# A graph layer with 34 wider node updates and some source columns copied on chip

## The chip, the cores and the metric

The kernel runs on one core of a Trainium2 chip. Its engines are TensorE (PE, with its weight load shown as PEld), VectorE (DVE), ScalarE (ACT), GpSimd (POOL) and SyncE (SP, which issues most transfers). The metric is the device time of one execution in microseconds, median of the runs.

## What is computed

A message-passing layer over 12,500 nodes of 64 values and 200,000 edges with 32 values each, in fp32. The edges come sorted by destination; destinations are drawn as 12500·u² with u uniform, so nodes with small numbers have many edges and those with large numbers few.

```python
msg_in = concatenate([nodes[row], nodes[col], edge_features])     # row: source, col: destination
messages = relu(msg_in @ mW1 + mb1) @ mW2 + mb2                   # hidden width 128, result 64
aggregated = segment_sum(messages, col)
upd = relu(concatenate([nodes, aggregated]) @ uW1 + ub1) @ uW2 + ub2
out = layernorm(nodes + upd)
```

## The kernel before

**Tables.** mW1 has three parts, for source, destination and edge. The products of all nodes with the first two are made once, in 13 chunks each: `chunk_a` writes `tab_a` = x·W1a to DRAM (L408 to L422) at the start, and `chunk_b` writes `tab_b` = x·W1b + b1, its first part at the start and the rest within the loop.

**Tiles and groups.** 128 edges are a tile (1563 of them), eight tiles a group (196, counted by `s`), two groups a pair (98, counted by `g`). The loop over `s` is at L583; the order of its work is written out by hand (`tc.manual_schedule()`), and each engine works in the order in which its instructions were issued there.

**What a group costs.** In each step of the loop:

- `gather` (L164, POOL): one indirect DMA per tile fetches 128 rows of 512 bytes of `tab_a` by the edges' sources. There are 14 buffers of a group (`ROWB`), so gathers are issued 14 groups ahead; the gather into a buffer waits for `h` of the group that used it. The first 8 groups (`XG`) gather rows of x instead.
- `windows` (L220, L225, SP): eight DMAs, each 32 rows of `tab_b`, for the destinations of a tile: they are sorted, so those of a tile lie within 32 nodes (`WIN`).
- `edge_part` (L251, PE): for each tile, one matmul adds the edges' own part and the destinations' part, by a stacked operand of 64 rows: edge values, and a 0/1 selection of the window's rows. In fp32 a matmul is shown as two passes.
- `node_part` (L272 DVE, L273 ACT): `h` = relu(pc + xg), eight tiles in one instruction each.
- `collect` (L298, L303, PE): the messages' hidden values are summed over destinations. For each tile `h` times a 0/1 matrix of 32 columns is added into the columns of `sums` at the tile's window, and edges are counted into `cnt`. The place comes from a register, loaded at L294.
- `select`, `load`, `counts`, `loadd` (L190 to L211): the 0/1 matrices for the pair after, and its edge values.

**Node updates.** `sums` covers 384 nodes (`UW`). When the edges of a stretch of nodes are done, an update follows, spread over some steps: `close` copies sums and counts to SBUF (ACT, L317 and L318), `columns` loads the nodes' x columns (SP, L324 and L326), `carry` takes the window that two stretches share over into the next sums (PE, L311 and L312), `update` multiplies to 128 hidden values (PE L333 and L334, ACT L336), `residual` multiplies back and takes the statistics (PE L344 and L345, DVE L349 and L351, ACT L353), `norm` scales (DVE L359 and L362), and `store` writes (SP L368). Which updates there are is fixed ahead by `updates()` from the expected distribution: 54 of them, each ending at a whole pair. `offsets` works out at the start where each tile's window lies in its stretch.

**In case of other data.** A flag is computed from the real destinations (`checks`); where a window or a stretch would be too wide, a slow general path at L627 does everything again.

Of the kernel before, what the change touches and what calls it, by code (L numbers as in the profile page):

```python
# [11 lines left out]
I32 = mybir.dt.int32  # L12
# [28 lines left out]
EARLY = NCH * P  # L41
GE = 20
BS = 8
UB = 3
NCOL = (-(-N // P) + UB) * P
UW = UB * P
ONE = D - 1


def updates():  # L50


    def node(g):
        return N * min(1.0, g * SUP * P / E) ** 2
    at = [0]
    for g in range(1, NSUP):
        if g > at[-1] and node(g + 1) - node(at[-1]) > UB * P - 2 * WIN:
            at.append(g)
    return at


# [1 line left out]


@with_exitstack
def gnn_kernel(ctx: ExitStack, tc: tile.TileContext, x1T, x, eT, e_rows, src, dst, dst_row, wrow, wnext, whalf,
               mW1, mb1, mW2, mb2, uW1, ub1, uW2, ub2, out):

# [35 lines left out]
    past = const.tile([1, 1], F32, name="past")  # L104
    w1b = const.tile([P, DH], F32, name="w1b")
    b1 = const.tile([P, DH], F32, name="b1")

    sums_s = [const.tile([P, UW], F32, name=f"sums_s{k}") for k in range(2)]
    xw = [const.tile([P, UW], F32, name=f"xw{k}") for k in range(2)]
# [21 lines left out]
    cps = cpool.tile([P, WIN + SUP], F32, name="cps")  # L131
    slot = cps[:, :WIN]
    drc = const.tile([P, NT], F32, name="drc")
    flag_i = const.tile([1, 1], I32, name="flag_i")
    usup = const.tile([1, K], I32, name="usup")
    ustep = const.tile([1, K], I32, name="ustep")
# [4 lines left out]

    rows = ctx.enter_context(tc.tile_pool(name="rows", bufs=ROWB))
    xg = {}

    def frees(s):

# [6 lines left out]
    def gather(s):  # L153

        if s >= XG or s % 2 == 0:
            buf = rows.tile([P, SUB, DH], F32, name="xg")
        else:
            buf = xg[s - 1][0]
        if s < XG:
            a = buf.rearrange("p k (b d) -> p (k b) d", d=D)[:, s % 2 * SUB:(s % 2 + 1) * SUB, :]  # L160
        else:
            a = buf.rearrange("p (b k) d -> p k b d", b=2)
        for i, t in enumerate(tiles(s)):
            nc.gpsimd.indirect_dma_start(  # L164
                out=a[:, i, :] if s < XG else a[:, i // 2, i % 2, :], out_offset=None, in_=A[:, :] if s >= XG else x[:, :],
                in_offset=bass.IndirectOffsetOnAxis(ap=src_s[:, t:t + 1], axis=0))
        xg[s] = buf, a

    with tc.tile_pool(name="sup", bufs=2) as sup, tc.tile_pool(name="work", bufs=2) as work, tc.manual_schedule():
# [63 lines left out]
            nc.scalar.copy(xt, pt)  # L233
            xs[s] = xt

        def parts(n):

            if n == SUB:
                return [slice(0, SUB)]
            return [slice(b * SUB // 2, b * SUB // 2 + (n - b + 1) // 2) for b in range(2) if n > b]  # L240

        def edge_part(s):

            n = len(tiles(s))
            g, j = divmod(s, SUP // SUB)
            pc = psum.tile([P, 2, SUB // 2, DH], F32, name="pc")
            for i in range(n):
                k, b = divmod(i, 2)
                q, m = 64 * b, j * SUB // 2 + k

                nc.tensor.matmul(pc[:, b, k, :], L[g][q:q + 64, m, :], rhs[g % 2][q:q + 64, m, :],  # L251
                                 start=s >= XG or k == 0, stop=s >= XG)
            pcs[s] = pc

        def node_part(s):

            n = len(tiles(s))
            pc = pcs.pop(s)
            h = work.tile([P, 2, SUB // 2, DH], F32, name="h")
            if s < XG:  # L260
                xt = xs.pop(s)
                for i in range(n):
                    k, b = divmod(i, 2)
                    q = 64 * b
                    nc.tensor.matmul(pc[:, b, k, :], xt[q:q + 64, k, :], w1a[q:q + 64], start=False,
                                     stop=i + 2 >= n)
                nc.scalar.activation(h, pc, AF.Relu)
            else:
                hf, pf = (t.rearrange("p b k f -> p (b k) f") for t in (h, pc))
                a = xg.pop(s)[0]  # L270
                for m in parts(n):
                    nc.vector.tensor_tensor(hf[:, m], pf[:, m], a[:, m], op=ALU.add)  # L272
                    nc.scalar.activation(hf[:, m], hf[:, m], AF.Relu)  # L273
            hs[s] = h

        def opened(u):
# [37 lines left out]
        def close(u):  # L314

            ps, pn = sums.pop(u)
            nc.scalar.copy(sums_s[u % 2], ps)  # L317
            nc.scalar.copy(xw[u % 2][0:1], pn)  # L318

        us = {}  # L320

        def columns(u):

            n0 = nc.values_load(usup[0:1, u:u + 1], engines=[ET.SP], min_val=0, max_val=N - 1,  # L324
                                skip_runtime_bounds_check_because="destinations are node numbers")
            nc.sync.dma_start(xw[u % 2][ONE:], x1T[:, bass.ds(n0, UW)])  # L326
            us[u] = n0

        def update(u):

            n0 = us[u]
            pu = psum.tile([DH, UW], F32, name="pu", tag="pc")
            nc.tensor.matmul(pu, w2u, sums_s[u % 2], start=True, stop=False)  # L333
            nc.tensor.matmul(pu, uz, xw[u % 2], start=False, stop=True)  # L334
            hT = work.tile([DH, UW], F32, name="hTu", bufs=1)
            nc.scalar.activation(hT, pu, AF.Relu, bias=ub1_s)  # L336
            us[u] = (n0, hT)

        def residual(u):

            n0, hT = us[u]
# [23 lines left out]

        def store(u):
            n0, o = us.pop(u)
            nc.sync.dma_start(out[bass.ds(n0, UW), :].rearrange("(c p) d -> p c d", p=P), o)  # L368


        WCH = 1024

        def relative(a, b):

# [57 lines left out]
        def offsets():  # L432

            nc.vector.memset(usup[:, 0:1], 0)
            wv = wint.rearrange("o (g t) -> o g t", t=SUP)
            ov = woff.rearrange("o (g t) -> o g t", t=SUP)
            k = 0
            while k < K:
                end = UPD[k + 1:] + [NSUP]
# [7 lines left out]
                nc.vector.tensor_tensor(o, w, usup[:, k:k + n].unsqueeze(2).broadcast_to([1, n, d * SUP]),  # L447
                                        op=ALU.subtract)
# [22 lines left out]
        for t in xw:  # L471
# [11 lines left out]
        for k, c in enumerate(range(0, NB, NCH)):  # L483
# [14 lines left out]
            if k == 9:  # L498
                select(0)
                load(0)  # L500
                counts(0)
        columns_of(NCH, nc.sync)

        def rest(s):

            if s == 1:
                relative(8 * SUP, 8 * SUP + WCH)
            elif s == 2:
                relative(8 * SUP + WCH, NT)
                halves(4 * SUP, NTP // 2)  # L510
            elif s == BS:
# [31 lines left out]
        def checks():  # L543
# [17 lines left out]

            uf = work.tile([1, K + 1], F32, name="uf", bufs=1)
            nc.vector.tensor_copy(uf[:, :K], usup)
            nc.vector.memset(uf[:, K:], float(N - WIN))
            gap = work.tile([1, K + 1], F32, name="gap", bufs=1)
            nc.vector.tensor_tensor(gap[:, :K], uf[:, 1:], uf[:, :-1], op=ALU.subtract)
            nc.vector.tensor_scalar(gap[:, :K], gap[:, :K], float(UB * P - WIN), None, op0=ALU.is_gt)
# [4 lines left out]

        due = {SUP // SUB * (UPD[u + 1] if u + 1 < K else NSUP) + 1: u for u in range(K)}
        last = SUP // SUB * NSUP + 1

        period = [max(u for u in range(K) if UPD[u] * SUP <= s * SUB) for s in range(NSUB)]
        transpose(0)
        edge_part(0)  # L580
        gathered = XG
# [1 line left out]
        for s in range(last + 3):  # L583
# [9 lines left out]
                node_part(s)  # L593
            if 1 <= s <= NSUB:
                collect(s - 1)
            if j == 0 and g + 1 < NSUP:
                select(g + 1)
                load(g + 1)
# [190 lines left out]
```

## Time and profile before

| | |
|---|---|
| runs | 2796.53, 2772.33, 2795.54 us; median 2795.54 |
| profiled execution | 2797.45 us, span 2795.7 us |
| instructions counted as work | PE 9558 (and as many weight loads), DVE 1103, ACT 534, POOL 1572 |
| busy share of the span | PE 59%, PEld 51%, DVE 20%, ACT 13%, POOL 53% |
| gathers of `tab_a` (L164) | 1499, 944 ns each, 1415.0 us busy |
| moved | 213.70 MB, 76 GB/s over the span |
| granted TensorE clock | 0.54 of full speed |
| gathers of `tab_a` begin | 138.6 us |

A line of the costliest groups reads: line of the code, engine, operation, output<-inputs, how many; then busy time and mean duration of one in ns; then the idle time of the engine just before them with what ended most of it. "Issue" is time in which the engine waited for nothing that the profile shows. Busy shares are means over the whole span: the start (tables), the long loop with gathers and its last part without gathers have different limits.

### The profile page before, as it was taken

To read this page: it belongs to the slowest core of one execution; us is meant where nothing else is said; L and a number is where in the kernel's file an instruction comes from. 1 tells how busy PE (TensorE), PEld (TensorE's weight loads), DVE (VectorE), ACT (ScalarE), POOL (GpSimd) and SP (SyncE) were. 2 spreads that over 40 slices of the span, in tenths; PEclk is the share of its full clock that TensorE was granted. 3 is DMA by queue.
4 is the path that set the end of the run, shared out by engine and by line. 5 is a ranking of instruction groups with operands and counts; after the bars stand their busy time and mean duration, and the time that the engine had idled before them with its cause. 6 is when DMAs were issued, how large, how long until landed. Compare 5 with 4: busy or idle time off the path is not lost. (4 is left out here: it accounts for less than half of the span.)

```text
span 2795.7 us, 34750 instructions
## 1 busy us (share of the span) xinstructions
PE 1650.0 (59%) x9558; PEld 1427.7 (51%) x9558; DVE 553.1 (20%) x1103; ACT 361.6 (13%) x534; POOL 1476.6 (53%) x1572
## 2 busy tenths in 40 slices
PE   1412755555564646655656655656666676675788
PEld 1312654555454545544546544555555555564667
DVE  0200121222111112111211211212122222221233
ACT  0100101101010111111111111111111111111122
POOL 7175445654555655555555564565555555555510
PEclk6555555555555555555555555555555555555566
DMA  3531233333222222222222222222222222222221
GB/s 89 144 90 51 74 84 91 90 93 85 69 75 67 78 67 73 74 72 72 74 73 74 73 75 71 70 77 76 71 76 66 77 75 75 75 78 73 74 69 44
DMA packets 248063, 213.70 MB, mean 76 GB/s; under 512 B 81153, under 2 KB 213143, under 8 KB 247880
## 3 DMA queue, kind: packets, MB, share of 16 engines
q0 software_dynamic: 50016, 100.44, 14.0%
q1 hardware_dynamic: 182310, 100.72, 13.1%
q10 hardware_dynamic: 15554, 10.31, 1.3%
q8 instruction: 90, 1.47, 0.2%
q14 instruction: 93, 0.76, 0.1%
HBM read 192.55 MB, written 18.68 MB: 76 GB/s over the span
## 5 line engine op out<-in xcount | busy, mean ns | idle before, releaser
L164 POOL DMA_INDIRECT xg<-tab_a,src_s x1499 | 1415.0, 944 | 1183.8 <-DVE h L272 440.6
L251 PE MATMUL pc<-rhs,l 64*128 64x128 f32 x3126 | 531.4, 424 | 677.5 <-issue 411.8
L251 PEld LDWEIGHTS pc<-rhs,l 64*128 64x128 f32 x3126 | 432.1, 306 | 733.9 <-issue 629.4
L298 PEld LDWEIGHTS sums<-sel,h 128*128 128x128 f32 x3126 | 637.2, 301 | 206.6 <-issue 199.8
L298 PE MATMUL sums<-sel,h 128*128 128x32 f32 x3126 | 626.8, 366 | 151.7 <-issue 149.8
L272 DVE TENSOR_TENSOR h<-pc,xg 128x1024 f32<-128x1024 f32 x189 | 228.6, 1210 | 954.5 <-remote 319.5
L273 ACT ACTIVATE h<-h 128x1024 f32<-128x1024 f32 x189 | 197.7, 1047 | 598.9 <-DVE h L272 495.3
L196 DVE TENSOR_TENSOR sel<-cps,drc 128x512 f32<-128x512 f32 x98 | 67.3, 686 | 634.6 <-remote 333.4
L192 DVE TENSOR_TENSOR l<-l,cps 128x1024 f32<-128x1024 int32 (+1 forms) x101 | 123.3, 1221 | 206.0 <-DMA l<-in_dst_row 159.6
L204 ACT CAST selb<-sel 128x512 bf16<-128x512 f32 x98 | 60.4, 616 | 667.4 <-DVE sel L196 398.4
L303 PE MATMUL cnt<-selb,one 128*1 128x32 bf16 x1563 | 95.2, 188 | 51.0 <-issue 50.6
L336 ACT ACTIVATE hTu<-pu,ub_s 128x384 f32<-128x384 f32 x54 | 31.3, 580 | 696.0 <-remote 308.5
L344 PE MATMUL py<-ux,xw 128*128 128x64 f32 x324 | 95.5, 384 | 26.7 <-issue 23.1
L303 PEld LDWEIGHTS <-one 128*1 128x1 bf16 x1563 | 62.7, 83 | 89.7 <-issue 77.5
L345 PE MATMUL py<-u,hTu 128*128 128x64 f32 x324 | 93.9, 382 | 21.1 <-issue 20.7
L344 PEld LDWEIGHTS py<-ux,xw 128*128 128x128 f32 x324 | 77.1, 288 | 34.3 <-issue 28.4
L345 PEld LDWEIGHTS py<-u,hTu 128*128 128x128 f32 x324 | 79.8, 297 | 26.0 <-issue 25.5
L408 PE MATMUL pb<-w1a,xl 64*128 64x128 f32 x196 | 30.6, 430 | 99.6 <-DMA xl<-in_x1T 93.2
L333 PE MATMUL pu<-sums_s,w2u 128*128 128x384 f32 x108 | 88.2, 921 | 1.5 <-ACT sums_s L317 1.5
L408 PEld LDWEIGHTS pb<-w1a,xl 64*128 64x128 f32 x196 | 26.2, 311 | 103.7 <-issue 92.8
L334 PE MATMUL pu<-xw,uz 128*128 128x384 f32 x108 | 73.7, 782 | 0.0
L349 DVE BATCH_NORM_STATS2 st<-py 128x6 f32<-128x64 f32 x162 | 26.6, 220 | 237.6 <-PE py L345 120.3
(86 smaller groups left out, 594.3 us busy)
## 6 DMA issues: line engine op xcount, KB each, us to landing
l<-in_dst_row SPq DMA_DIRECT2D x196, 128.0 KB
l<-in_eT SPq DMA_DIRECT2D x196, 128.0 KB
rhs<-tab_b SPq DMA_DIRECT2D x1563, 16.0 KB
xg<-tab_a,src_s POOLq DMA_INDIRECT x1499
tab_b<-tb SPq DMA_DIRECT2D x13, 512.0 KB
tab_a<-tb ACTq DMA_DIRECT2D x12, 512.0 KB
xw<-in_x1T SPq DMA_DIRECT2D x54, 97.5 KB
out<-o SPq DMA_DIRECT2D x54, 96.0 KB
```

The lines of the kernel that those rows point to most:

```text
L164: nc.gpsimd.indirect_dma_start(out=a[:, i, :] if s < XG else a[:, i // 2, i % 2, :], out_offset=None, in_=A[:, :] if s >= XG else x[:, :], ...
L192: nc.vector.tensor_tensor(l[r], l[r].bitcast(I32), node[r].unsqueeze(2).broadcast_to([r.stop - r.start, SUP // 2, P]), op=ALU.is_equal)
L196: nc.vector.tensor_tensor(s[:, :nt], slot.unsqueeze(1).broadcast_to([P, nt, WIN]), drc[:, g * SUP:g * SUP + nt].unsqueeze(2).broadcast_to( ...
L251: nc.tensor.matmul(pc[:, b, k, :], L[g][q:q + 64, m, :], rhs[g % 2][q:q + 64, m, :], start=s >= XG or k == 0, stop=s >= XG)
L272: nc.vector.tensor_tensor(hf[:, m], pf[:, m], a[:, m], op=ALU.add)
L273: nc.scalar.activation(hf[:, m], hf[:, m], AF.Relu)
L298: nc.tensor.matmul(ps[:, bass.ds(ws[i], WIN)], h[:, i % 2, i // 2, :], S[g][:, k0 + i, :], start=False, stop=ends and i == n - 1)
L303: nc.tensor.matmul(pn[:, bass.ds(ws[i], WIN)], one, SB[g][:, k0 + i, :], start=False, stop=ends and i == n - 1)
L333: nc.tensor.matmul(pu, w2u, sums_s[u % 2], start=True, stop=False)
L334: nc.tensor.matmul(pu, uz, xw[u % 2], start=False, stop=True)
L344: nc.tensor.matmul(py[:, i], xw[u % 2][:, i * P:(i + 1) * P], ux, start=True, stop=False)
L345: nc.tensor.matmul(py[:, i], hT[:, i * P:(i + 1) * P], u2, start=False, stop=True)
```

## The change

Two things are changed.

**Updates.** They cover 448 nodes (`UN`) instead of 384, may end at any group instead of at whole pairs, and there are 34 instead of 54: after groups 35, 49, 60, 69 and so on; every four groups from 128 to 160, every three from there to 193. `sums` and the counts are 480 columns wide (448 and a window), the columns behind are worked on in four blocks of 128, not three. `close` is issued earlier in the step, ahead of `edge_part`.

**Copied tiles.** x, transposed, is kept in SBUF whole (`xcol`, 64 partitions of 12,544 columns, loaded by seven DMAs at the start). In each odd full group from 13 on, 91 groups, the last tile is not gathered. Instead `copies` brings the x columns of its 128 sources one by one into a tile `xo`, 64 in each of two steps: 36 by copies of one column on ACT, 28 by adds of one column and a zero on DVE. Each address is a register value; they are loaded by two multi-register loads on ACT (18 each) and one on DVE (28). `edge_part` then adds xo·W1a for this tile with one more matmul, and `node_part` adds over seven tiles and makes the relu of the eighth directly from `pc`, as an ACT instruction of its own.

```diff
-UB = 3
+CG = 2
+CF = 6 * CG
+CA = 36
+NCT = -(-(NSUB - CF) // CG)
+UB = 4
-UW = UB * P
+UN = 448
+UW = UN + WIN
...
-        for i, t in enumerate(tiles(s)):
+        for i, t in enumerate(tiles(s)[:SUB - copied(s)]):
             nc.gpsimd.indirect_dma_start(
...
+    def copied(s):
+        return s >= CF and s % CG == CG - 1 and len(tiles(s)) == SUB
...
                 nc.tensor.matmul(pc[:, b, k, :], L[g][q:q + 64, m, :], rhs[g % 2][q:q + 64, m, :],
-                                 start=s >= XG or k == 0, stop=s >= XG)
+                                 start=s >= XG or k == 0, stop=s >= XG and not c)
+                if c:
+                    nc.tensor.matmul(pc[:, b, k, :], xo[s // CG % 2][q:q + 64], w1a[q:q + 64], start=False, stop=True)
...
-                for m in parts(n):
+                for m in parts(n, copied(s)):
                     nc.vector.tensor_tensor(hf[:, m], pf[:, m], a[:, m], op=ALU.add)
                     nc.scalar.activation(hf[:, m], hf[:, m], AF.Relu)
+                if copied(s):
+                    nc.scalar.activation(h[:, 1, SUB // 2 - 1], pc[:, 1, SUB // 2 - 1], AF.Relu)
...
+        def copies(s):
+            t = (s + 2) // CG * CG + CG - 1
+            if t < CF or not t < NSUB or not copied(t):
+                return
+            n = P // CG
+            k = (s + 2) % CG * n
+            r = t // CG - CF // CG
+            to = xo[t // CG % 2]
+            def by_dve(o, i):
+                nc.vector.tensor_tensor(o, i, slot[D:, 0:1], op=ALU.add)
+
+            parts = []
+            for a, b, e, copy in ((k, k + CA // 2, ET.Activation, nc.scalar.copy),
+                                  (k + CA // 2, k + CA, ET.Activation, nc.scalar.copy),
+                                  (k + CA, k + n, ET.DVE, by_dve)):
+                _, v = nc.values_load_multi_w_load_instructions(
+                    srow[r:r + 1, a:b], engines=[e], min_val=0, max_val=N - 1,
+                    skip_runtime_bounds_check_because="sources are node numbers")
+                parts += [(copy, a + i, v[i]) for i in range(b - a)]
+            for copy, i, v in parts:
+                copy(to[D:, i:i + 1], xcol[D:, bass.ds(v, 1)])
...
-            nc.sync.dma_start(xw[u % 2][ONE:], x1T[:, bass.ds(n0, UW)])
+            nc.sync.dma_start(xw[u % 2][ONE:, :UN], x1T[:, bass.ds(n0, UN)])
...
+        XCH = 2048
+        def xload(c):
+            e = min(c + XCH, NB * P)
+            nc.sync.dma_start(xcol[D:, c:e], x1T[1:, c:e])
...
                 counts(0)
+                for c in range(0, NB * P, XCH):
+                    xload(c)
...
             if 1 <= s <= NSUB:
                 collect(s - 1)
+            if s + 1 in due:
+                close(due[s + 1])
...
                 chunk_b(chunks.pop(0), [Bv])
+            copies(s)
             if s + 1 < NSUB:
...
-            if s + 1 in due:
-                close(due[s + 1])
             if s + 2 in due:
                 columns(due[s + 2])
```

More of the change, by code (lines that the diff above doesn't have):

```diff
@@ L43, with node @@
 BS = 8
-UB = 3
+CG = 2
[3 more added lines that the diff above has]
+UB = 4
 NCOL = (-(-N // P) + UB) * P
-UW = UB * P
+UN = 448
+UW = UN + WIN
 ONE = D - 1
 def updates():
-    def node(g):
-        return N * min(1.0, g * SUP * P / E) ** 2
+    def node(s):
+        return N * min(1.0, s * SUB * P / E) ** 2
     at = [0]
-    for g in range(1, NSUP):
-        if g > at[-1] and node(g + 1) - node(at[-1]) > UB * P - 2 * WIN:
-            at.append(g)
+    for s in range(1, NSUB):
+        if s > at[-1] and node(s + 1) - node(at[-1]) > UN - WIN:
+            at.append(s)
     return at
@@ L65, in gnn_kernel @@
 @with_exitstack
-def gnn_kernel(ctx: ExitStack, tc: tile.TileContext, x1T, x, eT, e_rows, src, dst, dst_row, wrow, wnext, whalf,
+def gnn_kernel(ctx: ExitStack, tc: tile.TileContext, x1T, x, eT, e_rows, src, src_row, dst, dst_row, wrow, wnext, whalf,
                mW1, mb1, mW2, mb2, uW1, ub1, uW2, ub2, out):
@@ L106, in gnn_kernel @@
     b1 = const.tile([P, DH], F32, name="b1")
+    xcol = const.tile([P, NB * P], F32, name="xcol")
     sums_s = [const.tile([P, UW], F32, name=f"sums_s{k}") for k in range(2)]
-    xw = [const.tile([P, UW], F32, name=f"xw{k}") for k in range(2)]
+    xw = [const.tile([P, UB * P], F32, name=f"xw{k}") for k in range(2)]
+    hT = const.tile([DH, UB * P], F32, name="hTu")
     rhs = [const.tile([P, SUP // 2, DH], F32, name=f"rhs{k}") for k in range(2)]
@@ L133, in gnn_kernel @@
     drc = const.tile([P, NT], F32, name="drc")
+    srow = const.tile([NCT, P], I32, name="srow")
+    xo = [const.tile([P, P], F32, name=f"xo{k}") for k in range(2)]
     flag_i = const.tile([1, 1], I32, name="flag_i")
@@ L234, in transpose, with parts @@
             xs[s] = xt
-        def parts(n):
+        def parts(n, last=False):
             if n == SUB:
-                return [slice(0, SUB)]
+                return [slice(0, SUB - last)]
             return [slice(b * SUB // 2, b * SUB // 2 + (n - b + 1) // 2) for b in range(2) if n > b]
@@ L249, in edge_part @@
                 q, m = 64 * b, j * SUB // 2 + k
+                c = copied(s) and i == n - 1
                 nc.tensor.matmul(pc[:, b, k, :], L[g][q:q + 64, m, :], rhs[g % 2][q:q + 64, m, :],
-                                 start=s >= XG or k == 0, stop=s >= XG)
+                                 start=s >= XG or k == 0, stop=s >= XG and not c)
+                if c:
+                    nc.tensor.matmul(pc[:, b, k, :], xo[s // CG % 2][q:q + 64], w1a[q:q + 64], start=False, stop=True)
             pcs[s] = pc
@@ L317, in close @@
             nc.scalar.copy(sums_s[u % 2], ps)
-            nc.scalar.copy(xw[u % 2][0:1], pn)
+            nc.scalar.copy(xw[u % 2][0:1, :UW], pn)
+        def copies(s):
[18 more added lines that the diff above has]
+                copy(to[D:, i:i + 1], xcol[D:, bass.ds(v, 1)])
         us = {}
@@ L331, in update @@
             n0 = us[u]
[L332 to L337, printed above, removed]
+            pu = psum.tile([DH, UN], F32, name="pu", tag="pc")
+            nc.tensor.matmul(pu, w2u, sums_s[u % 2][:, :UN], start=True, stop=False)
+            nc.tensor.matmul(pu, uz, xw[u % 2][:, :UN], start=False, stop=True)
+            nc.scalar.activation(hT[:, :UN], pu, AF.Relu, bias=ub1_s)
         def residual(u):
-            n0, hT = us[u]
+            n0 = us[u]
             py = psum.tile([P, UB, D], F32, name="py", tag="pc")
@@ L367, in store @@
             n0, o = us.pop(u)
-            nc.sync.dma_start(out[bass.ds(n0, UW), :].rearrange("(c p) d -> p c d", p=P), o)
+            nc.sync.dma_start(out[bass.ds(n0, UB * P), :].rearrange("(c p) d -> p c d", p=P), o)
+        XCH = 2048
         WCH = 1024
+        def xload(c):
+            e = min(c + XCH, NB * P)
+            nc.sync.dma_start(xcol[D:, c:e], x1T[1:, c:e])
         def relative(a, b):
@@ L434, in offsets @@
             nc.vector.memset(usup[:, 0:1], 0)
-            wv = wint.rearrange("o (g t) -> o g t", t=SUP)
-            ov = woff.rearrange("o (g t) -> o g t", t=SUP)
+            wv = wint.rearrange("o (s t) -> o s t", t=SUB)
+            ov = woff.rearrange("o (s t) -> o s t", t=SUB)
             k = 0
             while k < K:
-                end = UPD[k + 1:] + [NSUP]
+                end = UPD[k + 1:] + [NSUB]
                 d = end[0] - UPD[k]
@@ L446, in offsets @@
                 w, o = (v[:, UPD[k]:UPD[k] + n * d].rearrange("o (n d) t -> o n (d t)", n=n) for v in (wv, ov))
-                nc.vector.tensor_tensor(o, w, usup[:, k:k + n].unsqueeze(2).broadcast_to([1, n, d * SUP]),
+                nc.vector.tensor_tensor(o, w, usup[:, k:k + n].unsqueeze(2).broadcast_to([1, n, d * SUB]),
                                         op=ALU.subtract)
@@ L470, in gnn_kernel @@
         nc.vector.memset(zero_b, 0.0)
-        for t in xw:
+        for t in (*xw, hT):
             nc.vector.memset(t, 0.0)
@@ L508, in rest @@
             elif s == 2:
+                nc.sync.dma_start(srow, src_row[CF * SUB + SUB * CG - 1::SUB * CG, :][:NCT])
                 relative(8 * SUP + WCH, NT)
@@ L563, in checks @@
             nc.vector.tensor_copy(uf[:, :K], usup)
-            nc.vector.memset(uf[:, K:], float(N - WIN))
+            nc.vector.memset(uf[:, K:], float(N))
             gap = work.tile([1, K + 1], F32, name="gap", bufs=1)
             nc.vector.tensor_tensor(gap[:, :K], uf[:, 1:], uf[:, :-1], op=ALU.subtract)
-            nc.vector.tensor_scalar(gap[:, :K], gap[:, :K], float(UB * P - WIN), None, op0=ALU.is_gt)
+            nc.vector.tensor_scalar(gap[:, :K], gap[:, :K], float(UN), None, op0=ALU.is_gt)
             nc.vector.tensor_copy(gap[:, K:], past)
@@ L571, in checks @@
             nc.vector.tensor_tensor(flag_i, pf, bad, op=ALU.add)
-        due = {SUP // SUB * (UPD[u + 1] if u + 1 < K else NSUP) + 1: u for u in range(K)}
-        last = SUP // SUB * NSUP + 1
-        period = [max(u for u in range(K) if UPD[u] * SUP <= s * SUB) for s in range(NSUB)]
+        due = {(UPD[u + 1] if u + 1 < K else NSUB) + 1: u for u in range(K)}
+        last = NSUB + 1
+        period = [max(u for u in range(K) if UPD[u] <= s) for s in range(NSUB)]
         transpose(0)
@@ L771 @@
         "src": sp.reshape(-1, P).T[:, :NT],
+        "src_row": sp.reshape(-1, P),
         "dst": dp[:EPAD].reshape(-1, P).T[:, :NT],
```

## The prediction

> **What bounds the kernel now.** I read the costliest groups first, then the table by stretches of time, the waits, and last the timeline of one stretch. Nothing in this program is busy all the time, so the pace has to be found from what waits for what.
>
> ```profile
> L164 POOL DMA_INDIRECT xg<-tab_a,src_s x1499 | 1415.0, 944 | 1183.8 <-DVE h L272 440.6
> L251 PE MATMUL pc<-rhs,l 64*128 64x128 f32 x3126 | 531.4, 424 | 677.5 <-issue 411.8
> L298 PE MATMUL sums<-sel,h 128*128 128x32 f32 x3126 | 626.8, 366 | 151.7 <-issue 149.8
> ```
>
> Here the columns are busy time, mean of one, and idle time before with its releaser. The gathers are the largest single item. A gather lasts 0.944 us and is followed by 0.30 us of issue (timeline below), so one takes 1.245 us and a group of eight takes 10 us. POOL is busy or issuing for about 1415 + 443 = 1858 us. For 440.6 us it waits for h (L272) of the group whose buffer it wants, so POOL is not simply the bound: the wait is closed in a ring from POOL through the arithmetic back to POOL.
>
> ```profile
> core 0: us, PE busy (x) PEld busy (x) DVE busy (x) ACT busy (x) POOL busy (x), PEclk, DMA share, GB/s
> 1100.00:1700.00 600.00, 358.52 (x2008) 313.90 (x2007) 113.98 (x203) 75.72 (x106) 340.31 (x361) 0.52 0.27 73
> 1900.00:2680.00 780.00, 517.07 (x2849) 432.88 (x2849) 171.06 (x420) 118.37 (x196) 419.56 (x446) 0.57 0.28 74
> 2680.00:2776.00 96.00, 95.89 (x698) 79.95 (x696) 40.17 (x103) 28.36 (x49) 1.12 (x2) 0.73 0.23 63
> ```
>
> The last row is the important one: there the gathers have ended. The same table for h alone gives the number of groups in each stretch:
>
> ```profile
> 1100.00:1700.00 600.00, 54.86 (x45) 0.52 0.27 73
> 1900.00:2680.00 780.00, 68.21 (x56) 0.57 0.28 74
> 2680.00:2776.00 96.00, 16.46 (x15) 0.73 0.23 63
> ```
>
> So a group takes 600/45 = 13.3 us, then 780/56 = 13.9 us, and 96/15 = 6.4 us without gathers (I take 6.8, because the first groups of that stretch had been begun before it). The gathers cost the loop about twice what it needs without them. The two stretches with gathers hold 10 and 28 node updates, and differ by only 0.6 us per group.
>
> ```profile
> PEld pc L251 <- issue: 629.4, 395, 21.1
> POOL xg L164 <- issue: 442.6, 1434, 1.0
> POOL xg L164 <- DVE h L272: 440.6, 67, 16.0
> PE pc L251 <- issue: 411.8, 333, 8.1
> ...
> 2618.61 0.37 PE L251 MATMUL pc<-rhs,l 64*128 64x128 f32 x1 [0.22 <-issue]
> 2620.08 0.37 PE L251 MATMUL pc<-rhs,l 64*128 64x128 f32 x1 [1.10 <-issue]
> 2621.55 0.37 PE L251 MATMUL pc<-rhs,l 64*128 64x128 f32 x1 [1.10 <-issue]
> 2619.12 0.94 POOL L164 DMA_INDIRECT xg<-tab_a,src_s  x1 [0.30 <-issue]
> 2625.04 0.71 SPq L326 DMA_DIRECT2D xw<-in_x1T  x1
> ```
>
> The waits give total, times and longest; the timeline gives start, duration, and the idle time in brackets. While gathers run, PE stands still for "issue": its passes come 1.47 us apart, that is 0.71 us for each of the two instructions (weight load and matmul), and SP moves at the same 0.71 us. Reading the timeline through, such slow stretches fill about half of the time while gathers run (some 6.4 us per group), and none comes after the last gather. **The gathers are therefore the bound twice**: by their own pitch and by holding up PE and SP.
>
> **Removed: 91 gathers.** Odd groups from 13 to 193 lose one gather of eight; 91 of 1499. What is one worth? If POOL's pitch counted in full, 1.245 x 91 = 113 us. If POOL would only wait longer for h, nothing. From the table: (13.6 - 6.8)/8 = 0.85 us for each gather of a group, with the effect on PE and SP inside. I take this: 91 x 0.85 = **-77 us**, ends 0 and -113.
>
> **Removed: 20 updates; those left are wider.** An update has 4 blocks, not 3. PE pays L333 and L334 twice each per update, (921 + 782) x 2 = 3.4 us at 384 columns, about 4.0 at 448 by their length, and 6 x 0.38 = 2.3 us of L344 and L345, then 3.1 us. That is 54 x 5.7 = 308 us of PE against 34 x 7.1 = 241 us: 67 us less PE. But the group's time hardly follows the updates: 0.50 against 0.22 per group in the two stretches, and 0.6 us between them, so at most 2.1 us per update; and the stretch of 340 to 1100 us, with 4 updates, takes 13.8 us per group, as much as the last. I take 0.25 us for each: **-5 us**; ends 0 and -67. Moving `close` ahead of edge_part on ACT has one answer: sums are ready there, and its two copies (463 ns each) come before the relu of the next group: nothing. The carried window, the 480 columns of sums and 10 instead of 7 runs of offsets (at the start, small operations of DVE behind the table) are within 2 us together.
>
> **Added: the copies.** For each of 182 groups ACT gets 36 copies of one column and two register loads, DVE 28 adds and one load; besides, each needs its address worked out by the engine's sequencer. The trace has no such copy. Rows that are near: a load of 8 registers (L294) takes 0.59 us, of one (L308) 0.31, so 18 take about 1.0 and 28 about 1.4 us. For ACT the nearest short row is sd, 128x3, 296 ns, which is followed 0.20 us after its start by the next instruction:
>
> ```profile
> 2644.91 0.30 ACT L353 ACTIVATE sd<-mv,eps 128x3 f32<-128x3 f32 x1 [0.62 <-DVE mv L351]
> 2645.11 0.46 ACT L317 COPY sums_s<-sums 128x384 f32<-128x384 f32 x1
> 2645.47 0.46 ACT L318 COPY xw<-cnt 1x384 f32<-1x384 f32 x1
> L351 DVE BATCH_NORM_AGGREGATE mv<-st 128x2 f32<-128x6 f32 x162 | 16.1, 154 | 0.0
> ```
>
> For DVE it is bn_aggr (154 ns, started 0.08 us apart). The address step costs 0.115 us on PE with its matmul (L298) and 0.04 on SP, and can lie beside the copy before. So a copy on ACT costs between 0.10 and 0.32 us; I take 0.15: 36 x 0.15 + 2 x 1.0 = **7.4 us per group** beside the 1.7 us that ACT has (75.72/45). On DVE 0.13: 28 x 0.13 + 1.4 = **5.0 us** beside 2.5 (113.98/45).
>
> [...] No run here shows a copy of one column yet. [...] Their cover is the group's time; past it each microsecond costs 182 us. They are issued ahead of edge_part of the next group and are needed by that (one more matmul in two passes, 0.8 us per two groups, which takes the place of an eighth of the add on DVE) only in the second of the two calls. What stands behind them on ACT and DVE is the relu and the add of the next group, for which POOL and PE wait.
>
> **The tail.** In the last 14 groups, without gathers, the cover is 6.8 us. ACT needs 9.1 for 10 of these groups, about +2 us each, +20; three updates fewer but wider, 8 x 5.7 against 5 x 7.1: -10. Sum **+10 us**.
>
> **The start.** x columns, 64 x 12544 x 4 = 3.2 MB, are loaded by seven DMAs on SP ahead of the loop, where the first 150 us moved 117 GB/s at a DMA share of 0.44. They come beside the rest of the table's writing, and SP's eT load and windows queue behind them. Alone at that rate 27 us; hidden, 0. **+6 us**, ends 0 and 25. SBUF for it (50 KB per partition) has no time.
>
> **Sum**: 2797 - 77 - 5 + 10 + 6 = 2731 against the profiled execution (2797.45, span 2795.7); the median of the runs is 1.9 lower, so **2729 us**, 2.4% faster. Its own range, from the gather's price (-113 to -40) and the start: 2680 to 2775.
>
> **Rivals.**
> *ACT is paced like PE (slower).* ACT would issue about 82 instructions per group, close to PE's 90 (2008 matmuls and as many loads in 45 groups), and PE loses its 6.4 us per group to slow stretches. If these hold ACT too, some 9 instructions pass in 6.3 us at 0.71 us; the rest, 8.5 us by the rows, needs fast time: 6.3 + 8.5 = 14.8 us per group, +1.5 x 182 = +273, and the saved gathers no longer count: about **3075**. With 0.12 per copy it is 2880. It decides as soon as ACT's work exceeds 7.0 us outside the slow stretches. For it: PE and SP both crawl, so it is not one engine's trait. Against it: L351 in its runs of three has 0.0 us idle, and ACT's and DVE's short runs are never torn apart; but none of these is longer than ten, and PE too gets through some 40 instructions before it slows.
> *Gathers were hidden (same).* POOL already waits 440.6 us for h; with 91 x 1.245 us less it would wait 113 us longer, and the copies in the ring DVE-PE-POOL eat the rest: **2795**. Against it: the group's time halves without gathers.
> *Full worth (faster).* -113 and half of the updates' PE (-33), nothing lost at the tail: 2797 - 146 + 6 = **2657**.
> *The change does not do what it says*: with these sources and destinations, no update spans over 448 nodes (the widest step between two starts is 418), so the slow general path at L627 stays out; under 1%.
>
> **Chances.** Forecast 0.40, full worth 0.08, hidden 0.13, ACT paced 0.39. A measurement of this kernel can tell about 1%. Faster 0.46, same 0.13, slower 0.41. The range takes in all of the forecast, most of full worth and two thirds of the slower rival, up to where a copy costs about 0.13 us under slow stretches.
>
> **What would show it.** After the change: POOL x1408 gathers with the same 944 ns; 34 hTu; groups at 12.9 us in 1100 to 1700 us where I am right, 14 and more where ACT is paced. ACT's busy time per group 1.7 to about 7, DVE's 2.5 to about 6. Copies of ACT and DVE in the timeline without gaps of 0.71 us (right) or torn apart by "issue" (the slower rival). POOL's wait for h not over 440 us by more than 50; gathers of tab_a beginning at most 10 us later than 138.6 us. I am wrong if POOL waits for h in place of the gathers saved, or if h waits for ACT's and DVE's copies.

## The result: 5.9% slower, and the profile after

The changed kernel takes **2952.12 us** (2946.04 to 2954.01) against 2789.18, a ratio of **1.059** (1.053 to 1.065). The profiled execution has a span of 2949.3 us. The forecast was 2729 us and faster; what came is between the two figures of the rival "ACT is paced like PE" (2880 and 3075).

The later numbers need one distinction: on some chips, as in this result and in the profile of before, the traces have the slow stretches of 0.71 us per instruction and kernel before takes about 2790 us ("with slow stretches"), and on others the traces have practically none and before takes 1984 us ("without"); what tells them apart isn't known.

The chain of waits that ended last, first of before (by engine; it could be followed back only through the last 500 us), then of the changed kernel, and the changed kernel's costliest groups:

```profile
PE 12%; issue 4%; another core or an unknown queue 2%; DVE 1%; ACT 0%; DVEq 0%; DMA 0%
...
ACTq 35%; issue 27%; ACT 21%; PE 4%; POOL 3%; DVE 3%; another core or an unknown queue 3%; DMA 2%; SPq 1%; DVEq 1%; POOLq 0%
ACTq L355 26%; ACT xo L360 16%; ACTq L360 9%; POOL xg L178 3%; ACT h L290 3%; ACT selb L218 1%; DVE h L289 1%; PE sums L317 1%; PE pc L266 1%; DVE o L402 1%; DMA xl<-in_x1T 1%; SPq L239 1%; ACT sums_s L336 0%; DVE l L206 0%
...
L178 POOL DMA_INDIRECT xg<-tab_a,src_s x1408 | 1328.7, 944 | 1380.6 <-DVE h L289 573.0
L360 ACT COPY xo<-xcol 64x1 f32 x6552 | 750.5, 188 | 1366.9 <-issue 1360.0
L349 DVE TENSOR_TENSOR xo<-xcol,cps 64x1 f32<-64x1 f32 x5096 | 682.8, 159 | 567.1 <-issue 563.8
```

ACT was 13% busy before and had 0% of the chain. Now it and its sequencer (ACTq, which shows 364 register loads at L355 and, for the addresses, 6552 FUSED_REGOPS of 46 ns in the median at L360) hold over half of the chain, and much of "issue" is probably ACT's: the copies (L360) had 1360 us of it ahead of them. The register loads (L355) alone are 26%. POOL saved 86 us of gathers and waits 573.0 us for h (L289; before, L272) instead of 440.6. By stretch: the busy time of all engines, then h alone, whose number is the number of groups, and then what the copies on ACT waited for in each of these stretches (total, times, longest):

```profile
core 0: us, PE busy (x) PEld busy (x) DVE busy (x) ACT busy (x) POOL busy (x), PEclk, DMA share, GB/s
340.00:1100.00 760.00, 412.45 (x2577) 367.46 (x2577) 368.44 (x1839) 315.76 (x2178) 408.95 (x435) 0.51 0.30 80
1100.00:1700.00 600.00, 329.31 (x1987) 289.48 (x1987) 271.12 (x1411) 252.99 (x1702) 305.16 (x324) 0.51 0.25 68
1900.00:2680.00 780.00, 409.16 (x2384) 350.52 (x2386) 319.31 (x1676) 304.35 (x1969) 348.30 (x370) 0.52 0.23 61
...
340.00:1100.00 760.00, 67.28 (x58) 0.51 0.30 80
1100.00:1700.00 600.00, 49.67 (x43) 0.51 0.25 68
1900.00:2680.00 780.00, 57.77 (x50) 0.52 0.23 61
...
ACT xo L360 <- issue: 397.4, 257, 6.3
ACT xo L360 <- issue: 314.4, 236, 5.3
ACT xo L360 <- issue: 424.3, 346, 5.3
```

A group takes 13.1, then 14.0, then 15.6 us (before: 13.8, 13.3, 13.9). Early it is shorter than before, as forecast; then it grows. The waits per group grow with it: 397.4/58 = 6.9, 314.4/43 = 7.3, 424.3/50 = 8.5 us. The timeline of ACT shows what they are made of:

```profile
1406.16 3.02 ACT L360 COPY xo<-xcol 64x1 f32 x29 [1.61 <-issue]
1409.41 0.29 ACT L360 COPY xo<-xcol 64x1 f32 x2 [0.23 <-issue]
1410.10 0.19 ACT L360 COPY xo<-xcol 64x1 f32 x1 [0.40 <-issue]
1410.83 0.29 ACT L360 COPY xo<-xcol 64x1 f32 x2 [0.55 <-issue]
1412.22 0.29 ACT L360 COPY xo<-xcol 64x1 f32 x2 [1.09 <-issue]
```

29 copies go at 0.10 us each, untouched; then single ones and pairs come 0.7 or 1.4 us apart, and DVE's adds at this time do the same (single ones start at 1413.67, 1414.39 and 1415.14 us). Of the 182 runs of 36 copies 151 are torn in this way, 132 of them already after 10 to 19 copies. The sum for ACT per group, from the trace (own work and copies, which are its busy time, the wait ahead of the first copy, which is mostly the loads, and the gaps between copies):

| stretch | own | copies | loads | gaps | sum | group |
|---|---|---|---|---|---|---|
| 340 to 1100 us | 1.5 | 4.0 | 4.8 | 2.1 | 12.4 | 13.1 |
| 1100 to 1700 us | 1.7 | 4.2 | 4.4 | 2.9 | 13.2 | 14.0 |
| 1900 to 2680 us | 1.8 | 4.3 | 3.9 | 4.6 | 14.6 | 15.6 |

ACT is full to some 94%. Of the 153.6 us by which the two spans differ, 7.5 lie ahead of the first gather of the table (146.1 against 138.6 us), 103.1 between that and the last gather (2791.1 less 146.1, against 2680.5 less 138.6), and 43.0 behind it.

### The profile page after: what moved, and what is told of

Read it like the earlier page. It is cut to its first block, busy times and chain, and to the rows that moved or that the text cites. A ratio compares the mean times of both kernels' runs of the same rounds, so it can differ in the third digit from the quotient of the medians.

```text
span 2949.3 us, 58348 instructions
## 1 busy us (share of the span) xinstructions
PE 1547.1 (52%) x9436; PEld 1348.7 (46%) x9436; DVE 1212.4 (41%) x6108; ACT 1089.3 (37%) x7097; POOL 1390.3 (47%) x1481
## 3 DMA queue, kind: packets, MB, share of 16 engines
q0 software_dynamic: 47104, 94.47, 12.4%
## 4 chain that ended last, share of the span: by engine, by line
ACTq 35%; issue 27%; ACT 21%; PE 4%; POOL 3%; DVE 3%; another core or an unknown queue 3%; DMA 2%; SPq 1%; DVEq 1%; POOLq 0%
ACTq L355 26%; ACT xo L360 16%; ACTq L360 9%; POOL xg L178 3%; ACT h L290 3%; ACT selb L218 1%; DVE h L289 1%; PE sums L317 1%; PE pc L266 1%; DVE o L402 1%; DMA xl<-in_x1T 1%; SPq L239 1%; ACT sums_s L336 0%; DVE l L206 0%
## 5 line engine op out<-in xcount | busy, mean ns | idle before, releaser
L178 POOL DMA_INDIRECT xg<-tab_a,src_s x1408 | 1328.7, 944 | 1380.6 <-DVE h L289 573.0
L360 ACT COPY xo<-xcol 64x1 f32 x6552 | 750.5, 188 | 1366.9 <-issue 1360.0
L349 DVE TENSOR_TENSOR xo<-xcol,cps 64x1 f32<-64x1 f32 x5096 | 682.8, 159 | 567.1 <-issue 563.8
L266 PE MATMUL pc<-rhs,l 64*128 64x128 f32 x3126 | 431.5, 428 | 376.8 <-issue 111.3
L266 PEld LDWEIGHTS pc<-rhs,l 64*128 64x128 f32 x3126 | 362.0, 315 | 406.1 <-issue 123.5
L289 DVE TENSOR_TENSOR h<-pc,xg 128x1024 f32<-128x1024 f32 (+1 forms) x189 | 217.2, 1150 | 320.5 <-DMA xg<-tab_a,src_s 175.7
L269 PE MATMUL pc<-w1a,xo 64*128 64x128 f32 x182 | 64.4, 455 | 370.3 <-ACT xo L360 324.9
L290 ACT ACTIVATE h<-h 128x1024 f32<-128x1024 f32 (+1 forms) x189 | 188.1, 996 | 124.0 <-DVE h L289 91.7
L269 PEld LDWEIGHTS pc<-w1a,xo 64*128 64x128 f32 x182 | 46.2, 312 | 390.7 <-ACT xo L360 341.7
L375 PE MATMUL pu<-sums_s,w2u 128*128 128x448 f32 x68 | 63.3, 1034 | 147.2 <-ACT h L292 85.8
```

What stands on the lines that cost most here:

```text
L178: nc.gpsimd.indirect_dma_start(out=a[:, i, :] if s < XG else a[:, i // 2, i % 2, :], out_offset=None, in_=A[:, :] if s >= XG else x[:, :], ...
L269: nc.tensor.matmul(pc[:, b, k, :], xo[s // CG % 2][q:q + 64], w1a[q:q + 64], start=False, stop=True)
L349: nc.vector.tensor_tensor(o, i, slot[D:, 0:1], op=ALU.add)
L360: copy(to[D:, i:i + 1], xcol[D:, bass.ds(v, 1)])
```

## Experiments

My theory after this result: ACT is the bound, by its register loads and by copies that the slow stretches tear apart. Rivals: the updates cost the time; DVE's adds do, since h queues behind them; the gathers are still the bound. Ratios are to before on the same chip.

| run | what | slow stretches | us | ratio, 95% |
|---|---|---|---|---|
| u_only | updates alone | without | 1980.83 | 0.998 (0.998 to 0.999) |
| g_nocopy | 91 tiles neither gathered nor copied | without | 1869.12 | 0.943 (0.941 to 0.944) |
| k_allgathers | copies made, all tiles gathered | without | 2078.64 | 1.048 (1.046 to 1.049) |
| s_static | copies from fixed columns, no loads | without | 1872.09 | 0.943 (0.942 to 0.945) |
| after2 | the change | with | 2963.85 | 1.061 (1.054 to 1.068) |
| l_loads | as g_nocopy, see below | with | 2633.07 | 0.941 (0.935 to 0.948) |
| cg4_both | one tile of four groups, both engines | with | 2781.22 | 0.998 (0.994 to 1.002) |
| cg4_dve | one tile of four groups, DVE alone | with | 2765.52 | 0.990 (0.983 to 0.996) |
| d_off2 | without DVE's share | without | 2071.64 | 1.043 (1.042 to 1.045) |
| a_off2 | without ACT's share | without | 1870.11 | 0.943 (0.941 to 0.944) |
| after4 | the change | without | 2075.53 | 1.046 (1.044 to 1.047) |
| cg4_dve2 | as cg4_dve | without | 1933.14 | 0.974 (0.972 to 0.975) |
| cg3 | one tile of three groups, both engines | without | 2111.22 | 1.064 (1.063 to 1.066) |

**The first four: which part of the change costs?** u_only:

```diff
     def copied(s):
-        return s >= CF and s % CG == CG - 1 and len(tiles(s)) == SUB
+        return False
...
-                for c in range(0, NB * P, XCH):
-                    xload(c)
...
-                nc.sync.dma_start(srow, src_row[CF * SUB + SUB * CG - 1::SUB * CG, :][:NCT])
```

> The 34 wider updates alone; no tile is copied, and x columns and sources are not loaded for it. Theory (the loss comes from ACT and DVE, by register loads and by copies that the slow stretches pace): the updates are worth a little, -5 us in the loop and -11 in the tail, about 2775 us or 0.994 of before. Rival (the wider updates and the earlier close cost the time): most of the loss is here already, 2880 us or more.

g_nocopy (xo set to zero once):

```diff
-            if t < CF or not t < NSUB or not copied(t):
-                return
+            return
```

> The changed kernel with 91 tiles neither gathered nor copied (their x part is left out; xo is zero, its matmul stays). Gives the worth of a gather when nothing replaces it. Prediction's price of 0.85 us: 77 us below the updates alone, about 2700 us. Full pitch of 1.245: about 2665. Gathers hidden behind the wait for h: no different from the updates alone, about 2775.

k_allgathers:

```diff
-        for i, t in enumerate(tiles(s)[:SUB - copied(s)]):
+        for i, t in enumerate(tiles(s)):
```

> The changed kernel, all tiles gathered as before and the copies made all the same. Theory (ACT's copies are the bound, gathers matter only by the slow stretches they make): 10 to 40 us above the changed kernel, about 2980 us. Rival (gathers are still the bound and the copies only add a wait in the ring): +77 us or more, 3030.

s_static:

```diff
-                _, v = nc.values_load_multi_w_load_instructions(
-                    srow[r:r + 1, a:b], engines=[e], min_val=0, max_val=N - 1,
-                    skip_runtime_bounds_check_because="sources are node numbers")
+                v = [(s * P + i) * 37 % N for i in range(a, b)]
...
-                copy(to[D:, i:i + 1], xcol[D:, bass.ds(v, 1)])
+                copy(to[D:, i:i + 1], xcol[D:, v:v + 1])
```

> The changed kernel with the copies' columns fixed numbers in the program: as many copies, but no register loads and no address steps, so the 91 tiles get wrong sources. Theory with the weight on loads and address steps (4.2 us of loads per group stand on the chain of waits): falls below before, about 2740 us. Theory with the weight on the copies as instructions in slow stretches: half of the loss stays, 2860 us or more.

The numbers in these texts were too high in level, since without slow stretches before takes 29% less time; the ratios answer. In u_only POOL waits for practically nothing; its largest wait and two lines of its timeline:

```profile
POOL xg L178 <- issue: 463.7, 1521, 0.3
...
1199.56 0.94 POOL L178 DMA_INDIRECT xg<-tab_a,src_s  x1 [0.30 <-issue]
1200.81 0.94 POOL L178 DMA_INDIRECT xg<-tab_a,src_s  x1 [0.30 <-issue]
```

Only the 0.30 us of issue is left. Here POOL is the bound, plainly. A gather less is then worth (1980.83 - 1869.12)/91 = 1.23 us, its full pitch. The updates are worth 3 us. Copies from fixed columns cost nothing: 1872 against 1869 us. With the loads and address steps, and all gathers made, it is 2079: above u_only, so something beyond POOL is the bound. The rival "updates" is out for this condition, and so is "gathers still the bound": after4 has 91 gathers less than k_allgathers and differs by 3 us.

**The same change on the chip with slow stretches, and copying less.** after2 is the changed kernel. l_loads was meant to keep the loads and leave out the copies:

```diff
-            for copy, i, v in parts:
-                copy(to[D:, i:i + 1], xcol[D:, bass.ds(v, 1)])
```

but nothing reads the registers then, and its trace has no load from srow. It is read as g_nocopy with slow stretches. cg4_both spreads a tile's copies over four groups with one load on each engine; cg4_dve gives all of them to DVE:

```diff
-CG = 2
+CG = 4
...
-CA = 36
+CA = 16            # cg4_dve: 0, and only the DVE line below
...
-            for a, b, e, copy in ((k, k + CA // 2, ET.Activation, nc.scalar.copy),
-                                  (k + CA // 2, k + CA, ET.Activation, nc.scalar.copy),
+            for a, b, e, copy in ((k, k + CA, ET.Activation, nc.scalar.copy),
                                   (k + CA, k + n, ET.DVE, by_dve)):
```

> The changed kernel itself again, to have it on the chip of the experiments. In the last runs before took 1984 us with gathers back to back and no slow stretches, so the loss must be weighed under both conditions. Theory (ACT is the bound by its two loads, 5.5 us, 36 copies, 3.75 us, and its own 1.7 us: 10.9 us per group): where there are no slow stretches, the same 2070 us as with all gathers kept, since a gather less then saves nothing, 1.045 of before. Rival (part of the gathers' worth still counts): 1990 us. With slow stretches: 2952 us, as before.

> The changed kernel with the register loads alone: the single-column copies are left out (xo is zero, so the x part of 91 tiles is missing). Theory (loads and copies add up on ACT): 5.5 + 1.7 = 7.2 us per group on ACT, under the 9.4 us of gathers, so no loss, about 1870 us where there are no slow stretches; with them about 2740. Rival (the loads by themselves stall ACT for longer, the relu queues behind them): over 1950 (2850).

> One tile of each four groups copied, 32 columns a step: 16 by ACT and 16 by DVE, with one load each. 46 to 48 gathers less than before. ACT needs about 1.5 + 1.7 + 1.7 = 4.9 us per group. Theory: hidden; 44 x 1.22 = -54 us against the updates alone: about 1928 us without slow stretches, 0.972 of before; with slow stretches 0.985 to 1.0 (fewer instructions than a run that outlasts the fast part). Rival (any copies in the ring cost a wait): 1980 or more.

> As the last, with all 32 columns of a step on DVE, by one load of 32, and ACT left as in the updates alone. DVE needs 2.1 + 32 x 0.134 + 2.5 = 8.9 us per group. Theory: still below the gathers' 9.7, but h can stand behind 6.4 us of copies: 1928 to 1960 us without slow stretches; with them slower than the version on both engines.

With slow stretches, too, leaving out gathers without a replacement gains (0.941), and the copies with their loads turn this into 1.061: 331 us, 1.8 us for each of 182 groups. At half the rate the loss is gone. The chains of after2, l_loads and cg4_dve, in this order, as far as they could be followed, have ACT and its sequencer only where ACT carries its full share:

```profile
ACTq 32%; issue 29%; ACT 19%; PE 6%; DVE 4%; POOL 2%; another core or an unknown queue 1%; DVEq 1%; DMA 1%; SPq 1%; POOLq 0%
...
PE 33%; issue 20%; SPq 5%; DMA 4%; another core or an unknown queue 3%; DVE 1%; POOL 1%; ACT 0%; DVEq 0%; POOLq 0%; ACTq 0%
...
issue 36%; DVE 18%; SPq 13%; DVEq 10%; PE 9%; another core or an unknown queue 5%; DMA 4%; POOL 4%; ACT 1%; ACTq 0%; POOLq 0%
```

In cg4_dve it is DVE and its sequencer that have 28% of the chain. That DVE alone does better than both engines (0.990 against 0.998) speaks against the rival that h behind DVE's adds is the cost; my own expectation said the reverse. There is a stronger sign: cg4_dve puts 32 adds per group on DVE, more than the changed kernel's 28, and gains all the same. Had each of its 42 gathers saved as much as the 91 of l_loads did (159 us with the updates), it would gain 73 us; it gains 26, so DVE's share costs some 47 us by this estimate, against the 331 of both shares.

**Which engine?** a_off2 and d_off2 leave out one engine's lines of the loop over parts (load and copies), as marked behind the lines; the columns concerned stay zero.

```diff
             for a, b, e, copy in ((k, k + CA // 2, ET.Activation, nc.scalar.copy),     # a_off2: out
                                   (k + CA // 2, k + CA, ET.Activation, nc.scalar.copy),     # a_off2: out
                                   (k + CA, k + n, ET.DVE, by_dve)):     # d_off2: out
```

> The changed kernel without DVE's share: its load and 28 of 64 columns are left out (they stay zero); ACT's two loads and 36 copies stay. Theory (ACT is the bound): nearly all of the loss stays, 1.04 with slow stretches, 1.04 without. Rival (h behind DVE's copies delays POOL and PE): falls to 0.98 or less.

> The changed kernel without ACT's share: its two loads and 36 of 64 columns are left out; DVE's load and 28 adds stay. Theory (ACT is the bound): most of the loss is gone, 0.96 with slow stretches, 0.945 without. Rival (DVE's share costs as much): 1.00 or more.

> The changed kernel. With slow stretches 1.06, as twice measured. Without: theory (ACT bound, gathers hidden): like k_allgathers and d_off2, 1.04 to 1.05. Rival: 1.00.

Without slow stretches it is ACT's share alone: d_off2 has the whole loss (1.043; after4 1.046) and a_off2 none of it (0.943, as g_nocopy). ACT's sum in after4, made as above, is 1.6 own, 3.8 copies, 4.3 loads and 0.1 gaps: 9.7 of a group's 10.0 us (760 us, 76 groups), where POOL needs 9.4 (7.5 gathers at the pitch of 1.25 us). Over 150 groups (the 21st to the 171st h) a group takes 10.28 us in after4, 9.99 in u_only and 9.28 in a_off2. The timeline of after4:

```profile
1216.24 3.72 ACT L360 COPY xo<-xcol 64x1 f32 x36 [4.13 <-issue]
1219.99 0.63 ACT L377 ACTIVATE hTu<-pu,ub_s 128x448 f32<-128x448 f32 x1
```

All 36 copies run in one piece; the 4.13 us ahead of them is the register loads. In s_static, without address steps, a run of 36 copies takes 3.4 us instead of 3.7 to 4.0, so the steps cost 0.6 us at most. Here the price is the loads, not the copies.

d_off3 (1.045), a_off3 (0.942), s_static3 (0.942), u_only3 (0.998) and u_only4 (0.999) repeat these, again without slow stretches. The labels u_only2, s_static2, d_off and a_off have no result.

**A version that wins, and one by the account that doesn't.**

> One tile of four groups, all 32 columns of a step on DVE. With slow stretches it gave 0.990. Without: DVE needs 2.1 + 32 x 0.134 + 2.5 = 8.9 us per group against 9.7 of gathers, so the 42 gathers less count in full: -51 us against the updates alone, 0.972. Rival (h waits behind the copies): 0.99 or more.

cg4_dve2 gives 0.974 as expected: POOL again waits for little but issue (443.3 us, at most 0.3 at a time), and 42 gathers less than u_only save 48 us. So this version beats both kernels in both conditions, by little with slow stretches (0.990 and 0.974). cg3 tried to go further:

```diff
-CG = 2
+CG = 3
...
-CA = 36
+CA = 14
...
-NCT = -(-(NSUB - CF) // CG)
+NCT = (NSUB - CF) // CG
...
-            n = P // CG
+            n = -(-P // CG)
...
-            for a, b, e, copy in ((k, k + CA // 2, ET.Activation, nc.scalar.copy),
-                                  (k + CA // 2, k + CA, ET.Activation, nc.scalar.copy),
-                                  (k + CA, k + n, ET.DVE, by_dve)):
+            for a, b, e, copy in ((k, k + CA, ET.Activation, nc.scalar.copy),
+                                  (k + CA, min(k + n, P), ET.DVE, by_dve)):
```

> One tile of each three groups copied, 43 columns a step: 14 on ACT with one load, 29 on DVE with one load. 59 gathers less than before. Account: ACT 1.4 + 1.5 + 1.7 = 4.6 us per group, DVE 1.9 + 3.9 + 2.5 = 8.3 us, both under the 9.6 of gathers; 59 x 1.25 = -74 us against the updates alone, 1908 us, 0.961, where there are no slow stretches. Rival (any share on ACT delays the relu and costs): 0.974 or more. With slow stretches more copies per group are torn apart than in cg4_dve: 0.99 to 1.01.

It was far off: 1.064. The lines of its loads (minimum, median and maximum in ns), and of the loads in the changed kernel and in cg4_dve2:

```profile
L354 DVEq TENSOR_LOAD <-srow x177: 1854/6564/7842, 204.1 to 2067.2; - x177
L354 ACTq TENSOR_LOAD <-srow x177: 1230/3061/4441, 205.9 to 2068.9; - x177
...
L355 ACTq TENSOR_LOAD <-srow x364: 49/2199/5227, 349.6 to 2899.8; - x182
L355 DVEq TENSOR_LOAD <-srow x182: 1847/1894/2096, 350.5 to 2892.8; - x182
...
L353 DVEq TENSOR_LOAD <-srow x168: 2097/2140/2517, 252.6 to 1856.5; - x168
```

On DVE in cg3, 28 registers take 1.9 us in one call of three (the last of a tile, which has one column less), and 29 take 6.7 us in the other two. On ACT, 14 registers take 1.26 us in one call and 3.1 in two; in the changed kernel the first load of 18 takes 1.5 and the second 3.9 to 4.0 us. The order of fast and slow repeats with the place where the load begins in srow (medians of the loads at each place):

| kernel, engine, registers | begins at byte | us |
|---|---|---|
| changed, ACT, 18 | 0 and 256 | 1.5 |
| changed, ACT, 18 | 72 and 328 | 3.9 to 4.0 |
| changed, DVE, 28 | 144 and 400 | 1.9 |
| cg3, ACT, 14 | 0 | 1.26 |
| cg3, ACT, 14 | 172 and 344 | 3.1 |
| cg3, DVE, 28 | 400 | 1.9 |
| cg3, DVE, 29 | 56 and 228 | 6.7 |
| cg4_both, ACT and DVE, 16 | multiples of 64 | 1.0 to 1.1 |
| cg4_dve, DVE, 32 | multiples of 128 | 2.1 |

All starts at a multiple of 16 bytes are fast, with 0.06 to 0.09 us per register, and all others slow, with 0.22 to 0.23. The number of registers alone can't be it, since 18 and 14 on ACT come in both kinds. A kernel that only moves a start wasn't run, so this is a reading of many loads and not a test.

It accounts for cg3: DVE's loads average (1.9 + 2 x 6.7)/3 = 5.1 us where I had put 1.9. Part of a load runs while DVE is still busy; from 340 to 1900 us the trace has, per group, 2.6 us of DVE's own work, 3.7 of adds and 3.9 of idle time ahead of adds, 10.2 of a group's 10.5 us and more than POOL's 9.6 (7.67 gathers at 1.25). It also bears on the changed kernel, where the second load of ACT begins at such a slow place. At 1.5 us instead of 4.0 it would leave ACT with 9.7 - 2.5 = 7.2 us per group without slow stretches, an estimate from the loads above, and this is less than POOL's 9.4. No such kernel was run.

## Why the prediction was wrong, step by step

- **The bound** was read rightly as far as gathers left out without a replacement gain 6%, in g_nocopy and l_loads. The ring with the wait for h belongs to the slow stretches alone: without them, in u_only and g_nocopy, POOL waits for practically nothing but its own issue (463.7 and 443.5 us, at most 0.3 at a time). And gathers alone don't make the slow stretches, as u_only's 1499 gathers, 944 ns each as in before, ran without them.
- **A gather's worth (0.85 us)** was too small. Without slow stretches it is 1.23, measured: POOL's full pitch, which the prediction had only as an end. With them, l_loads saves 159 us for 91 gathers and 20 updates, up to 1.7 us each; the split wasn't measured. In the stretch from 340 to 1100 us, which had only 4 updates before, l_loads has 60 groups against 55, 1.1 us per group for half a gather, with some 0.2 us of uncertainty as a count is good to one. Fewer gathers also came with fewer slow stretches (PE's idle time for "issue" is 663 us in l_loads, 707 in before), which the price by division had only in part.
- **The updates (-5 us, and -10 at the tail)**: 3 us in all without slow stretches. Right that PE's 67 us are nearly all hidden there. With slow stretches it stays open.
- **The copies at nothing: the step that failed.** What was put at nothing while gathers run costs, the tail included, 331 us with slow stretches (after2 against l_loads) and 206 without (after4 against g_nocopy). The zero was my own estimate: ACT was to need 7.4 + 1.7 = 9.1 us per group, which fits under a cover of 13.3; in the profile it is 12.4 to 14.6, where l_loads, with neither loads nor copies, takes 12.8 for a whole group (over the same 150 groups as above). Two terms are wrong. The loads: 2 x 1.0 us per group on ACT, taken from a line through loads of one and of eight registers (0.31 and 0.59 us); measured 1.5 + 4.0. And the question whether ACT is paced: I argued from runs of ten instructions that ACT isn't torn. At 36 copies and as many address steps it mostly is, in the same way as PE, with 2.1 to 4.6 us of gaps per group. A copy itself (0.10 us start to start and 188 ns long, so that copies in a row overlap) and an add (0.13) were sized well; the copy came in under the 0.15 taken.
- **The rival** "ACT is paced like PE" had the place and the sign, with 6.3 us of slow stretches per group and 2.0 us of loads; measured are 2.1 to 4.6 us of gaps and 3.9 to 4.8 of loads. The errors offset each other, so it was partly luck that its two figures held the result between them.
- **The tail (+10)** is +43. Without gathers no run of copies is torn (from 2791 us on, the idle time within one is 0.20 us at most), but the loads come uncovered: nine groups, by h from 2787.2 to 2885.1 us, take 10.9 us each against 6.8 before. ACT's 4.4 of loads, 3.8 of copies and 1.9 of its own work are about 10 of these; the loads were the mis-sized term again.
- **The start (+6)** is +7.5. The general path stayed out, as said.
- **The warning signs** came: POOL waits for h in place of the gathers saved (573 for 441 us), and a group takes 14.0 us from 1100 to 1700 us.

What stays open: how much of the loss with slow stretches is ACT's alone. The chains, ACT's sum and cg4_dve say most of it. The kernels that leave out ACT's or DVE's share alone were measured only without slow stretches, so the exact split isn't shown, nor whether the two shares cost more together than apart. Open is also what makes a chip show the slow stretches.

## What to carry to other kernels

Work handed to an idle engine as many tiny instructions cost that engine's sequencer here more than its datapath (ACTq 35% of the changed kernel's chain, ACT 21%; without slow stretches 4.3 us of loads per group against 3.8 of copies): sum its loads of registers, address steps and issue gaps against the group's time, and allow for a gap as soon as the run is longer than any in the trace. The register loads here grew with their count (on ACT 1.26 us for 14 and 1.5 for 18, on DVE 1.9 for 28 and 2.1 for 32) and differed with where they begin (on ACT 4.0 for 18 from byte 72 on); take their price from a load like it, at both kinds of start, before building on it. Leave an engine room below the bound: a half of the copies, on DVE only, filled it to an estimated 8.9 of 9.7 us and won, where the full number on two engines lost.

## What the hardware showed that I had not expected

- The same kernel takes 2790 us on one chip and 1984 on another. In the traces the difference is the slow stretches: in them an instruction of PE, SP, ACT or DVE starts about every 0.71 us. PE's idle time for "issue" is 707 us in before and 11 us in u_only, which ran without them.
- A load of 18 registers takes 1.5 us or 4.0, and one of 14 takes 1.26 or 3.1; in all loads of srow the fast ones begin at a multiple of 16 bytes.
- The instruction queue's packets grew from 93 to 281 (0.76 to 2.30 MB) with the copies; l_loads has 99. In after4, without slow stretches, they are 281 too, so their number isn't what brings the slow stretches.
